# A decoder layer in a planned instruction order: rank-16 projection in two passes, attention weights on ScalarE's queue, and a revised planner

## Chip, core and metric

One Trainium2 chip, one of its NeuronCores. The metric is the device time of one execution in microseconds. The kernel before was run three times: 1096.41, 1093.22 and 1092.48 us, median 1093.22 us. The profiled execution is a separate one.

## What is computed

The input is `x` (8 sequences of 512 tokens, 256 features) and a context of the same shape. Each of three sublayers is followed by a residual sum and a layernorm, cut here to what matters:

```python
# 1: chunked linear attention, chunks of 32, with a gate
S = einsum(Qc, Kc) * decay_mask;  O = einsum(S, Vc)
x = layernorm(x + (sigmoid(x @ W_g.T) * O @ W_o.T + x))
# 2: cross attention, 16 heads of 64, 512 queries on 512 keys
a = softmax((x @ Wq + bq)(ctx @ Wk + bk).T / 8);  o = a @ (ctx @ Wv + bv)
x = layernorm(x + o @ Wo + bo)
# 3: feed-forward with ternary weights and a rank-16 side path
h = bitlinear(x, w_fc) + gate * (x @ v.T @ fast_b.T @ u.T)
x = layernorm(x + bitlinear(relu(h) ** 2, w_proj))
```

The rank-16 projection is `x @ v.T` (256 features to 16).

## The kernel before

**Precision.** Every float32 operand of a matmul is kept as two float16 tiles, a high part and the rest. A product is made in three passes, high by high, high by low and low by high (`PASSES`, line 35; `mm`, line 472). Making the two halves is the bulk of the work of the other engines: ScalarE (ACT) casts the high part and VectorE (DVE) subtracts it, with GpSimd (POOL) taking some of each.

**Units.** Cross attention is cut into 256 units: batch `b` (8), head pair `p` (8), query block `qt` (4 of 128 queries). `scores` (line 1025) makes one unit: six `s` matmuls of 512 columns in three concurrent pairs, a DVE instruction per head that adds the mask and finds the row's extreme (`s`, `nm`), and an ACT exponential per head (`e`). `split_pe` (line 1057) makes the two float16 halves of the 128x1024 probabilities: the high half on ACT, or on POOL where `HIGH` has a "p" for this `qt` (first string for batch 0, second for the others), and the low half on DVE (`ph`, both halves in one of three buffers). `split_p` (line 1045) sends `ph` through a transposing DMA on SyncE's (SP's) queue into `pT` (five buffers). `attend` (line 1067) comes `LAG` = 4 units later and multiplies `pT` by the values: 24 `av` matmuls of 64 columns. A `ph` buffer is free again when its transpose has landed.

**Work between the units.** Generators yield the other work piece by piece, and a budget per unit (`PULL`) says how much is taken: key, query and value projections for later head pairs (`pk`, `pq`, `pvv`), the first sublayer of the next batch (`gen_l0`, from line 772), the output projection and feed-forward of the batch before (`gen_wo`, line 883, `gen_ffn`, line 938). In batch 0 the last is replaced by the preparation of the feed-forward weights (`setup_wo`, `setup_ffn`). In the feed-forward, `ffn_z` (line 918) makes the rank-16 projection `pz`: six matmuls of 512 columns into 128 PSUM rows, of which `zst` is made; `ffn_h` (line 927) then adds `ust` by `zst` to each of eight hidden blocks. `vst` holds the 16 columns of `v.T` at columns 0, 32 and 64, a tile each for high and low.

**Before the first unit.** `load_w0`, `load_decay`, the inputs of batch 0 and `load_qkv` (line 560) are issued on SP's queue in that order. `wqs`, six tiles of 512 KB, are the cross attention's weights; `setup_qkv` splits each in a 256-column and a 768-column piece. `setup_decay` (line 535) builds the decay mask: `ld` on ACT and DVE, then eight powers `pw` on POOL, then four DVE instructions `mdec`. The first sublayer of batch 0 follows from `xh0`, the halves of the input (`xs`), and from `w0`.

**What sets the order.** All of it is recorded first. `schedule` (line 280) then plays the recorded operations through a model with a duration for each (`cost`, line 235), picks for each engine, at each moment, the ready operation with the lowest due time, and emits the program in that order. Due times are the unit's number plus an offset per kind of work (`LATE`). `REACH` says how far ahead in due time DVE may reach for an operation that does not wait for the SBUF port it shares with POOL. The order is fixed when the program runs: each engine takes its instructions one after the other, and an instruction that waits holds those behind it.

**Completion counters.** In the built program each DMA reports to one of eight completion counters, given out in turn, and a DMA that gets a counter again waits first for the DMA that had it before.

All instructions are emitted from one line (414 before), so a profile row is told by its tile names.

Of the kernel before, what the change touches and what calls it, by code (L numbers as in the profile page):

```python
# [15 lines left out]
ALU = mybir.AluOpType  # L16
# [9 lines left out]
PSC = 2.0 ** 15  # L26
LAG = 4
MARGIN = 0.0
REACH = 5.83
SPARE = 1  # L30
HIGH = ("aaaa", "paaa")
LATE = {"k": 0.0, "q": 0.0, "v": 0.0, "w": 0.0, "l": -0.81, "o": -0.22, "f": 0.0, "s": 0.0, "a": 1.41}
PULL = {"k": 4.02, "l": 2.62, "w": 3.0, "f": 4.71, "g": 6.03}

PASSES = ((0, 0), (0, 1), (1, 0))

# [90 lines left out]

class Op:
    __slots__ = ("engine", "method", "args", "kw", "prio", "seq", "preds", "succs", "wait", "occ", "lat", "half", "port",
                 "bufs", "start", "end", "free", "ready", "parts")  # L130


class Engine:
# [12 lines left out]
class Recorder:  # L146
# [34 lines left out]
    def add(self, engine, method, args, kw):  # L181
        ins, outs = [], []
        for n, x in enumerate(args):
            if isinstance(x, View):
                (outs if n == 0 or (method == "tensor_tensor_reduce" and n == 7) else ins).append(x)
        for k, x in kw.items():
            if isinstance(x, View):
                (outs if k == "accum_out" else ins).append(x)
        o = Op()
        o.engine, o.method, o.args, o.kw, o.prio = engine, method, args, kw, self.prio  # L190
        o.preds, o.succs, o.bufs, o.parts = {}, [], [], None
# [12 lines left out]
        return o  # L204
# [30 lines left out]
    def cost(self, o, ins, outs):  # L235

        n = max([int(np.prod(x.shape[1:])) for x in outs + ins] or [0]) if o.engine != "PE" else outs[0].idx.size
        psum = any(x.t.pool[:2] == "ps" for x in ins + outs)
        ones = sum(x.idx.size == 1 and x.t.free > 0 for x in ins)
        o.half, o.port = None, o.engine == "POOL"  # L240
        if o.engine == "PE":
            o.occ = n / 2400 + 0.0025
            o.lat = o.occ + 0.17
            if ins[0].p1 - ins[0].p0 == 64:
                o.half = ins[0].p0
        elif o.engine == "DVE":
            lat = 0.145 + n * 1.042e-3
            if o.method == "tensor_tensor_reduce":
                o.occ, o.lat = 0.615, 0.8
                return  # L250
            if not psum and o.method in ("tensor_copy", "tensor_scalar") and n >= 512:
                lat = 0.12 + n * 0.62e-3
            if psum and ones and o.method == "scalar_tensor_tensor":
                lat += 0.065
            if n <= 8:
                lat = 0.19 if o.method == "reciprocal" else 0.175 if o.method == "bn_aggr" else 0.145
            o.occ, o.lat = lat - 0.085, lat
            o.port = not psum and o.method in ("tensor_tensor", "scalar_tensor_tensor", "tensor_scalar", "tensor_copy")
        elif o.engine == "ACT":
            lat = 0.165 + n * 0.83e-3 + (0.0 if psum else 0.04) + 0.07 * ones  # L260
            o.occ, o.lat = (lat + 0.01, lat + 0.12) if "accum_out" in o.kw else (lat - 0.11, lat)
        elif o.engine == "POOL":
            if o.method == "tensor_tensor":
                lat = 0.3 + n * 1.67e-3 if n <= 512 else 0.2 + n * 1.9e-3
                if o.args[3] == ALU.pow:
                    lat = 0.42 + 0.16 * n
            else:
                lat = 0.13 + n * 0.9e-3 if n > 512 else 0.62 if n > 256 else 0.56 if n > 8 else 0.22 + n * 5e-3
            o.occ, o.lat = lat - 0.03, lat
        else:  # L270
            x = (outs or ins)[0]
            if o.method == "dma_start_transpose":
                blocks = n / 128
                o.occ, o.lat = 0.1 * blocks + 0.4, 0.115 * blocks + 0.55
            else:
                size = {F32: 4, F16: 2}.get(x.t.dt, 1)
                o.occ, o.lat = 0.6, n * size * x.shape[0] / 200e3


    def schedule(self):  # L280
# [18 lines left out]
        dma, halved = 0.0, False  # L299
        port = {"DVE": 0.0, "POOL": 0.0}  # L300
        times = [0.0]
        for o in ops:
# [14 lines left out]
        while done < len(ops):  # L317
# [10 lines left out]
            while again:  # L328
                again = False
                for e in engines:  # L330
# [35 lines left out]
                    if e == "PE":  # L366
# [1 line left out]
                        st = now + (0.095 if halved and not grouped else 0.0)  # L368
                        halved = grouped
                        o.free, o.end = st + o.occ, st + o.lat  # L370
                    elif e == "SP":
                        st = max(now, dma - 1.5)
                        dma = max(st, dma) + o.lat
                        o.free, o.end = st + o.occ, max(dma, now + o.lat) + 2.1
                    else:
                        st = now
                        if o.port:
# [58 lines left out]
def decoder_kernel(ctx: ExitStack, tc: tile.TileContext, ins: dict, out: bass.AP):  # L436
# [26 lines left out]
    tfc = cst.tile([128, 2, HID], F16, name="tfc")  # L463
    tpj = cst.tile([128, 8, D], F16, name="tpj")
    ust = cst.tile([128, HID], F16, name="ust")
    vst = cst.tile([128, 2, 2, 128], F16, name="vst")
    sfc4 = cst.tile([128, 8], F32, name="sfc4")
    s2b = cst.tile([128, D], F32, name="s2b")
    bob = cst.tile([128, D], F32, name="bob")
# [129 lines left out]
    def setup_ffn():  # L599
# [445 lines left out]
    def split_p(u, e):  # L1045
# [148 lines left out]
    for i, u in enumerate(units):  # L1194
        b, p, qt = u
        if qt == 0:
# [17 lines left out]
        at(i, 0)  # L1214
        step(u)
        at(i, LATE["a"])
        while len(pend) >= LAG:
# [101 lines left out]
```

## Time and profile before

| | profiled execution |
|---|---|
| own time | 1087.98 us |
| span, first to last instruction | 1086.2 us |
| TensorE (PE) busy | 1016.7 us, 94%, 11986 matmuls |
| DVE busy | 995.6 us, 92% |
| ACT busy | 896.4 us, 83% |
| POOL busy | 542.0 us, 50% |
| DMA | 185.81 MB, mean 171 GB/s |
| mean granted PE clock | 0.991 |

The profiled execution took 1.8 us more than its span and 5.2 us less than the median of the three timed runs. Busy shares are means over stages with different limits. A matmul row's mean duration includes its pipeline; how fast matmuls follow each other is seen in rows such as `pk x6`, six of 512 columns in 1.29 us of the chain.

Stages can be told along the matmul row by counting `s` matmuls, 192 to a batch. The first unit's scores start at 49.4 us, those of batch 1 at 173.3, batch 2 at 298.9, batch 3 at 422.8, batch 4 at 548.7, batch 5 at 671.9, batch 6 at 797.4 and batch 7 at 920.2; the last unit's at 1032.2 us, and the span ends at 1086.2.

### The profile page before, as it was taken

The page shows a single profiled execution, that of the slowest core. Times are in us where ns is not written, and L with a number is a line of the kernel's source. Part 1 is how long each engine was busy: PE and PEld are TensorE (multiplying, and loading weights), DVE is VectorE, ACT ScalarE, POOL GpSimd, SP SyncE. Part 2 cuts the span into 40 slices and gives each one's busy share as a digit, 9 for nine tenths or more (in the row PEclk, how much of TensorE's full clock was granted, in tenths as well). Part 3 has the DMA queues.
Part 4 walks back from the last instruction along what each step waited for, and adds up shares of the span by engine and source line. Part 5 has one row for each costly group of instructions (what it writes and reads, how often), then busy time and mean ns, then how long its engine had stood idle before and what let it go on. Part 6 is the DMA issues. An engine that isn't in the chain of part 4 may idle for free.

```text
span 1086.2 us, 30429 instructions
## 1 busy us (share of the span) xinstructions
PE 1016.7 (94%) x11986; PEld 641.1 (59%) x11986; DVE 995.6 (92%) x2105; ACT 896.4 (83%) x1871; POOL 542.0 (50%) x508
## 2 busy tenths in 40 slices
PE   6987879999999999999999999999999999999976
PEld 4544545666566666665666665665666666564654
DVE  6999899999899989999898989999898999996987
ACT  6788788789877998789987898879987899788854
POOL 3332261256842587335951588435962567443335
PEclk9999999999999999999999999999999999999998
DMA  7389999999999999999999999999999999998961
GB/s 258 112 141 174 168 202 183 166 175 167 184 171 184 171 188 168 193 161 174 190 179 185 169 182 181 200 161 173 181 178 183 176 177 177 182 159 155 166 105 39
DMA packets 651791, 185.81 MB, mean 171 GB/s; under 512 B 633728, under 2 KB 646528, under 8 KB 651648
## 3 DMA queue, kind: packets, MB, share of 16 engines
q1 hardware_dynamic: 651648, 183.87, 94.8%
q8 instruction: 93, 1.52, 0.6%
q14 instruction: 50, 0.41, 0.1%
HBM read 21.04 MB, written 4.19 MB: 23 GB/s over the span
## 4 chain that ended last, share of the span: by engine, by line
PE 39%; DMA 19%; ACT 16%; DVE 15%; issue 5%; POOL 5%; SPq 1%; ACTq 0%; POOLq 0%; DVEq 0%
DMA pT<-ph 12%; PE s L414 7%; PE av L414 6%; ACT e L414 6%; PE pwo L414 5%; DVE ph L414 4%; DVE s L414 4%; PE pvv L414 3%; ACT ph L414 3%; PE ph L414 3%; DMA x2T<-xsb 3%; PE pq L414 3%; ACT r L414 3%; PE pk L414 3%; DMA oT<-oh 2%
## 5 line engine op out<-in xcount | busy, mean ns | idle before, releaser
L414 ACT ACTIVATE e<-s,nm 128x512 f32<-128x512 f32 x512 | 353.4, 697 | 79.9 <-DVE nm L414 72.2
L414 DVE CUSTOM_DVE_ANT_0 s<-s,mb 128x512 f32<-128x512 f32 x512 | 343.3, 707 | 30.2 <-PE s L414 25.9
L414 DVE SCALAR_TENSOR_TENSOR ph<-e,ph 128x1024 f16<-128x1024 f32 x256 | 336.9, 1317 | 20.5 <-ACT ph L414 15.8
L414 PEld LDWEIGHTS <-pT 128*128 128x128 f16 x6144 | 213.7, 98 | 94.8 <-issue 36.3
L414 PE MATMUL av<-v,pT 128*128 128x64 f16 x6144 | 233.4, 194 | 18.7 <-DMA pT<-ph 17.7
L414 ACT ACTIVATE ph<-e 128x1024 f16<-128x1024 f32 x200 | 214.2, 1073 | 25.5 <-DMA pT<-ph 20.8
L414 PE MATMUL s<-W 64*128 64x512 f16 x1536 | 219.7, 380 | 7.0 <-ACT e L414 4.8
L414 POOL TENSOR_SCALAR ph<-e 128x1024 f16<-128x1024 f32 x56 | 66.8, 1192 | 198.5 <-ACT e L414 157.9
L414 POOL TENSOR_TENSOR oh<-of,oh 128x512 f16<-128x512 f32 x63 | 90.9, 1442 | 120.1 <-ACT oh L414 117.1
L414 PEld LDWEIGHTS <-wqkv 128*128 128x128 f16 x768 | 67.7, 98 | 91.7 <-issue 31.5
L414 ACT ACTIVATION_READ_ACCUMULATOR e<-s,nm 128x1 f32 x512 | 108.6, 212 | 0.0
L414 PEld LDWEIGHTS <-W 64*128 64x128 f16 x1536 | 58.2, 94 | 80.7 <-issue 41.5
L414 POOL TENSOR_TENSOR rh<-r,rh 128x512 f16<-128x512 f32 x56 | 71.3, 1278 | 68.8 <-ACT rh L414 62.0
L414 PE MATMUL pk<-ctxh,wqkv 128*128 128x512 f16 x384 | 97.9, 379 | 2.1 <-POOL ctxh L414 0.9
L414 PE MATMUL pq<-x1T,wqkv 128*128 128x512 f16 x384 | 96.3, 383 | 3.7 <-ACT e L414 1.8
L414 PE MATMUL pvv<-wqkv,ctxh 128*128 128x256 f16 x768 | 96.1, 273 | 1.2 <-ACT e L414 1.2
L414 PE MATMUL pwo<-wo,oT 128*128 128x256 f16 x672 | 87.6, 273 | 3.4 <-DMA oT<-oh 3.4
L414 PEld LDWEIGHTS <-ctxh 128*128 128x128 f16 x768 | 70.8, 98 | 30.2 <-issue 17.6
L414 PEld LDWEIGHTS <-oT 128*128 128x128 f16 x768 | 70.7, 98 | 19.1 <-DMA oT<-oh 5.8
L414 DVE DVE_READ_ACCUMULATOR2_ANT nm<- 128x1 f32 x512 | 72.1, 141 | 0.0
L414 PE MATMUL ph<-x2T,tfc 128*128 128x512 f16 (+1 forms) x288 | 70.5, 361 | 0.1
L414 PE MATMUL py<-tpj,rh 128*128 128x256 f16 x448 | 60.6, 273 | 0.1
(186 smaller groups left out, 1501.3 us busy)
## 6 DMA issues: line engine op xcount, KB each, us to landing
row<-in_x SPq DMA_DIRECT2D x8, 512.0 KB, 5.4
pT<-ph SPq DMA_TRANSPOSE x255, 4.8
xs<-in_xT SPq DMA_DIRECT2D x7, 512.0 KB, 4.8
ctxs<-in_ctxT SPq DMA_DIRECT2D x7, 512.0 KB, 4.8
out_dram<-row SPq DMA_DIRECT2D x7, 512.0 KB, 3.4
wqs<-in_wqkv SPq DMA_DIRECT2D x6, 512.0 KB, 7.0
wos<-in_wo SPq DMA_DIRECT2D x4, 256.0 KB, 3.3
fcs<-in_w_fc SPq DMA_DIRECT2D x2, 512.0 KB, 4.2
```

The lines of the kernel that those rows point to most:

```text
L414: getattr(real[x.engine], x.method)(*[r(a) for a in x.args], **{k: r(a) for k, a in x.kw.items()})
```

## The change

1. `ffn_z`: `vst` becomes one tile with the high part of `v.T` at columns 0, 32 and 64 and the low part at 96. Each 128-column weight tile meets the high and the low half of the input once: four matmuls in place of six. `fbs`, from which `ust` is made, is copied to rows 96 too, so that the fourth group of 16 rows is summed in the same `ust` by `zst` matmul.
2. `load_qkv`: the six `wqs` transfers are issued by ACT's queue in place of SP's.
3. `HIGH` for batch 0: "papa" in place of "aaaa": the high half of `ph` is made on POOL for two of four query blocks.
4. The planner: new durations for DMAs and for one POOL operation, a limit of eight transfers in flight per queue, and new values of `REACH`, `LATE` and `PULL`. The transposes of `ph` get a due time of their own (`d`). Several new offsets are zero.

```diff
-REACH = 5.83
+REACH = 8.03
-HIGH = ("aaaa", "paaa")
-LATE = {"k": 0.0, "q": 0.0, "v": 0.0, "w": 0.0, "l": -0.81, "o": -0.22, "f": 0.0, "s": 0.0, "a": 1.41}
-PULL = {"k": 4.02, "l": 2.62, "w": 3.0, "f": 4.71, "g": 6.03}
+HIGH = ("papa", "paaa")
+LATE = {"k": 0.0, "q": 0.0, "v": 0.0, "w": 0.0, "l": -0.41, "o": -0.91, "f": 0.31, "s": 0.0, "a": 1.41, "t": 0.0, "x": 0.0, "e": 0.0, "c": 0.0, "d": -1.17}
+PULL = {"k": 4.02, "l": 2.62, "w": 3.05, "f": 4.71, "g": 6.26}
...
+        o.dma = o.method[:3] == "dma"
+        if o.dma:
+            x = (outs or ins)[0]
+            if o.method == "dma_start_transpose":
+                blocks = n / 128
+                o.occ, o.lat = 0.1 * blocks + 0.4, 0.115 * blocks + 0.55
+            else:
+                size = {F32: 4, F16: 2}.get(x.t.dt, 1)
+                o.occ, o.lat = 0.45, n * size * x.shape[0] / 300e3 + (1.2 if size == 1 else 0.1)
...
-                lat = ... 0.62 if n > 256 else ...
+                lat = ... 0.92 if n == 256 and o.kw == {} and o.method == "tensor_scalar" and o.args[-1] == ALU.is_lt else 0.62 if n > 256 else ...
...
-                o.occ, o.lat = 0.6, n * size * x.shape[0] / 200e3
...
-                    elif e == "SP":
-                        st = max(now, dma - 1.5)
+                    elif o.dma:
+                        st = max(now, landed[e][-8])
+                        if o.method == "dma_start_transpose":
+                            st = max(st, dma - 1.5)
                         dma = max(st, dma) + o.lat
-                        o.free, o.end = st + o.occ, max(dma, now + o.lat) + 2.1
+                        o.free, o.end = st + o.occ, max(dma, st + o.lat) + 2.2
+                        landed[e].append(o.end)
...
-    vst = cst.tile([128, 2, 2, 128], F16, name="vst")
+    vst = cst.tile([128, 2, 128], F16, name="vst")
...
-            nc.sync.dma_start(st, ins["wqkv"][i, c * 128:(c + 1) * 128])
+            nc.scalar.dma_start(st, ins["wqkv"][i, c * 128:(c + 1) * 128])
...
-        split(vst[:, :, 0, 0:RANK], vst[:, :, 1, 0:RANK], sv, WS)
+        split(vst[:, :, 0:RANK], vst[:, :, 96:96 + RANK], sv, WS)
         for g in (32, 64):
-            nc.vector.tensor_copy(vst[:, :, :, g:g + RANK], vst[:, :, :, 0:RANK])
+            nc.vector.tensor_copy(vst[:, :, g:g + RANK], vst[:, :, 0:RANK])
...
-        for g in (32, 64):
+        for g in (32, 64, 96):
             nc.vector.tensor_copy(fbs[:, :, g:g + RANK], fbs[:, :, 0:RANK])
...
-        mm(ps, lambda k, a: vst[:, k, a, :], lambda k, c: x2T[b][:, c, k, ts], 2)
+        for k in range(2):
+            for c in range(2):
+                nc.tensor.matmul(ps, vst[:, k, :], x2T[b][:, c, k, ts], start=(k == 0 and c == 0), stop=(k == 1 and c == 1))
...
+            nc.prio += LATE["d"]
             nc.sync.dma_start_transpose(t.rearrange("p a h k n -> p (a h k) n"), ph.rearrange("p a h n -> p (a h n)"))
+            nc.prio -= LATE["d"]
```

More of the change, by code (lines that the diff above doesn't have):

```diff
@@ L129 @@
     __slots__ = ("engine", "method", "args", "kw", "prio", "seq", "preds", "succs", "wait", "occ", "lat", "half", "port",
-                 "bufs", "start", "end", "free", "ready", "parts")
+                 "dma", "bufs", "start", "end", "free", "ready", "parts")
 class Engine:
@@ L190, in add @@
         o.engine, o.method, o.args, o.kw, o.prio = engine, method, args, kw, self.prio
+        if engine in ("DVE", "ACT") and method[:3] != "dma" and self.prio >= 0:
+            src = ins[0].t if ins else None
+            if method == "tensor_tensor_reduce":
+                o.prio += LATE["t"]
+            elif method == "activation" and args[2] == AF.Exp:
+                o.prio += LATE["x"]
+            elif src is not None and src.pool[:2] == "ps":
+                o.prio += LATE["e"]
         o.preds, o.succs, o.bufs, o.parts = {}, [], [], None
@@ L240, in cost @@
         o.half, o.port = None, o.engine == "POOL"
-        if o.engine == "PE":
+        o.dma = o.method[:3] == "dma"
[7 more added lines that the diff above has]
+                o.occ, o.lat = 0.45, n * size * x.shape[0] / 300e3 + (1.2 if size == 1 else 0.1)
+        elif o.engine == "PE":
             o.occ = n / 2400 + 0.0025
@@ L267, in cost @@
             else:
-                lat = 0.13 + n * 0.9e-3 if n > 512 else 0.62 if n > 256 else 0.56 if n > 8 else 0.22 + n * 5e-3
+                lat = 0.13 + n * 0.9e-3 if n > 512 else 0.92 if n == 256 and o.kw == {} and o.method == "tensor_scalar" and o.args[-1] == ALU.is_lt else 0.62 if n > 256 else 0.56 if n > 8 else 0.22 + n * 5e-3
             o.occ, o.lat = lat - 0.03, lat
[L270 to L276, printed above, removed]
-                o.occ, o.lat = 0.6, n * size * x.shape[0] / 200e3
     def schedule(self):
@@ L298, in schedule @@
         future = {e: [] for e in engines}
-        dma, halved = 0.0, False
+        dma, halved, landed = 0.0, False, {"SP": [0.0] * 8, "ACT": [0.0] * 8}
         port = {"DVE": 0.0, "POOL": 0.0}
@@ L1214, in decoder_kernel @@
         at(i, 0)
+        nc.prio = i + LATE["c"]
         step(u)
```

## Prediction

> **What bounds the kernel now.** I read the page's busy line and chain first, then the busy time of each engine by batch, the chain inside two batches, the waits of batch 0, and the timeline of the first 51 us.
>
> ```profile
> PE 1016.7 (94%) x11986; PEld 641.1 (59%) x11986; DVE 995.6 (92%) x2105; ACT 896.4 (83%) x1871; POOL 542.0 (50%) x508
> PE 39%; DMA 19%; ACT 16%; DVE 15%; issue 5%; POOL 5%; SPq 1%; ACTq 0%; POOLq 0%; DVEq 0%
> ```
>
> No engine has slack to speak of except POOL, and the chain is shared by four. So a microsecond saved on one engine is worth less than a microsecond.
>
> ```profile
> 0.00:49.40 49.40, 38.63 (x271) 24.16 (x273) 38.84 (x82) 32.29 (x63) 17.36 (x25) 1.00 0.62 204
> 49.40:173.30 123.90, 101.14 (x1182) 57.99 (x1182) 114.53 (x255) 101.74 (x219) 42.26 (x41) 0.97 0.97 166
> 298.90:422.80 123.90, 123.09 (x1481) 78.13 (x1478) 117.19 (x244) 106.29 (x223) 70.46 (x63) 1.00 1.04 178
> ```
>
> The columns are length, then busy time of PE, PEld, DVE, ACT and POOL, granted clock, DMA share and rate. Batch 2 is PE's: busy 123.1 of 123.9. Batch 0 is as long though PE is idle for 22.8 us in it; there DVE is nearest to full (114.5). The next lines show why, first the chain in batch 2, then in batch 0, then two waits of batch 0.
>
> ```profile
> 337.01 0.76 PE s L414 x6
> 337.76 1.40 PE pq L414 x6
> 339.16 1.29 PE pg L414 x6
> ```
> ```profile
> 56.73 6.37 DMA pT<-ph
> 63.18 1.06 ACT ph L414
> 70.92 6.25 DMA pT<-ph
> 77.25 1.06 ACT ph L414
> ```
> ```profile
> ACT ph L414 <- DMA pT<-ph: 7.2, 8, 1.5
> DVE ph L414 <- ACT ph L414: 3.4, 5, 1.1
> ```
>
> In batch 2 matmul follows matmul. In batch 0 a transpose of 6.4 us ends and an ACT cast starts: the cast needs one of three `ph` buffers, and ACT, waiting for it, holds its later exponentials. Last, the start:
>
> ```profile
> 0.72 1.28 ACT L414 ACT_TABLE_LOAD   x1 [0.72 <-PEq L1312]
> 5.20 0.20 ACT L414 ACTIVATE ld<-ld 128x1 f32<-128x1 f32 x1 [3.20 <-DMA ld<-in_log_decay]
> 5.77 8.73 POOL L414 TENSOR_TENSOR pw<-ld,dif 128x4 f32<-128x4 f32 x8 [4.95 <-DMA dif<-in_diffmask]
> 10.32 4.08 SPq L414 DMA_DIRECT2D wqs<-in_wqkv  x6
> 14.53 0.77 DVE L414 SCALAR_TENSOR_TENSOR mdec<-pw,dif 32x32 f32<-32x32 f32 x4 [1.96 <-POOL pw L414]
> 50.91 0.70 DVE L414 CUSTOM_DVE_ANT_0 s<-s,mb 128x512 f32<-128x512 f32 x1
> ```
>
> DVE waits 1.96 us for the decay powers and then works nearly without a stop to the first unit's scores at 50.91.
>
> **Two passes for three.** Fourteen matmuls of 512 columns go (two in each of seven batches) and four of 256. In the chain `pg x6` takes 1.29 us, so 0.215 each; half for 256. 14 x 0.215 + 4 x 0.108 = 3.4 us of PE. It counts in full where PE is the chain and not where DVE is: between 3.4 and nothing. Batches 1 to 6, where `pz` runs, are PE's by the table, so I take 2.6, three quarters. The extra copy of `fbs` is one DVE instruction of about 0.1 us, the smaller `vst` copies save less; nothing. If the cover of DVE work that stays (117.2 of 123.9 in batch 2) is the tighter bound, the term is zero.
>
> **The weights on ACT's queue.** Each issue costs about 0.5 us of an engine's queue (three `w0s` in 1.46 us of SP's timeline), so six leave SP and come to ACT, which has nothing to do before 5.20. The splits of `wqs`, between 18.85 and 43 us before, come first in ACT's new order, and the six pieces they feed on DVE go into DVE's idle time at the start: 10.6 us of idle in 49.4. That is the promise. Against it stands what is queued behind. In the changed order ACT issues the six first, then loads its table, then casts `wqs`, then `wqkh`, and only after five such casts `ld`. The built program gives its eight completion counters out over both queues, so ACT's sixth issue waits until the third `wqs` has landed, its fourth until `wqk` has, and SP's second `xs` until the first `wqs` has.
>
> When does the third `wqs` land? The first 20 us moved 293 GB/s at a DMA share of 0.86, so about 341 when full. `wqk`, 256 KB, took 3.1 us from issue to landing (the page's DMA list), of which 0.8 is its bytes: 2.3 fixed. Three `wqs` are 1.57 MB; with what SP issued beside them (two `wqk`, one `xs`) 2.36 MB. So it lands at 0.72 + 2.3 + 4.6 = 7.6 if ACT's transfers go first, 9.9 if all share. Another issue (0.5) and the table load (1.28) put ACT's first cast at 9.4 to 11.7, where `ld` was done at 5.20. From there DVE has 4.5 us of lower halves ahead of `ld` (five pieces of `wqs` and two of `wqkh` at their rows' durations) with 0.4 to start; then POOL's powers take 8.73, and `mdec` can start 13.7 after the first cast: 23.1 to 25.4. From `mdec` to the first unit's scores DVE has 67 instructions, 28.8 us at the rows' durations; before, the 70 there were 33.1 us of work in 36.4 us of time, so 3.3 were lost. I allow 2.7: 31.5. First scores at 54.6 to 56.9, against 50.91. In exchange 0.8 us of DVE work (`bob`, `fbs`) is done that came later before. The term is +2.9 to +5.2; I take +4. If the counters hold nothing and ACT starts at 5.2, the same sum gives 18.9 + 31.5 - 0.8 = 49.6: -1.3, the other end.
>
> Here a rule of the Trainium skill speaks against the edit. The rows just used say that the transfers of the start are limited by bytes: 5.9 MB in the first 20 us. "DMA: Bandwidth & Descriptors", section "Issuing engines are not separate DMA queues", says that DMAs run on the same 16 engines whoever starts them, and that issuing from several saves only the issue time. By the rule the landing would be the later of my two, the term +5.2 and the sum -0.7. The trace of before cannot show how two queues share, since only SP's was used.
>
> **POOL's casts in batch 0.** Sixteen high halves leave ACT (32.56 us for 31 casts in batch 0, so 1.05 each: 16.8 us of its 101.7) and come to POOL at 1.19 each (the `ph` row of POOL, 66.8 us for 56): 19.1 on 42.3, of 123.9, so POOL has room. ACT does not bound batch 0; DVE does, with 9.4 us idle. What ACT gains is that a cast waiting for a buffer waits on POOL, where nothing urgent is behind: half of 7.2 us of ACT's waits, and with them part of DVE's 3.4 for ACT. I take -3. The best is all of DVE's idle, -9.4. The worst: the cast is 0.14 us longer, 16 times 2.2, and DVE's `ph`, 37.25 us for 31 in batch 0 and 42.31 for 33 in batch 2, where POOL is busier, is stretched by 0.08 in 32 units, 2.6: +4.8.
>
> **Durations and dates.** In a middle batch the new order differs in 18 of DVE's 243 instructions, 9 of ACT's 158, 2 of POOL's 63 and 1 of SP's 47; the PE work between a unit's scores and its `av` is 17.3 us on average in both. So nothing structural moves. What such swaps do is bounded by what the kernel shows without any: batches 2 to 6, in one and the same order, took 122.8 to 125.9. I take 0, and 3.5 either way over the seven. In the tail (54.0 us) four short matmuls go and a few casts swap: -0.3. In the transposes' due time `d` I see no separate term: SP's order differs in one place of a batch.
>
> **Sum.** +4 - 2.6 - 3 + 0 - 0.3 = -1.9. Span 1086.2 to 1084.3, own time of the profiled execution 1087.98 to 1086.1, and of the median, which is 5.2 above that own time, 1093.2 to 1091.3.
>
> **Rivals.** (1) *Batch 0 gives up all its slack.* If the ring of three buffers with ACT in it is what keeps DVE at 114.5 of 123.9, taking ACT out of half the casts frees all 9.4 instead of 3: -8.3, 1084.9. For it: the transposes fill the chain of batch 0. Against: transposes still take 6.4 us and there are still three buffers.
> (2) *POOL holds DVE.* Both share a port to SBUF in the planner's model, and the timeline has a DVE `ph` of 1.93 us at 610.87 where 1.22 is usual. If each of 16 new POOL casts cost 0.71 on DVE, batch 0 would lose 11.4 instead of gaining 3: +12.5, 1105.7. It decides from the first cast on, since the other terms leave +1.1; at half the casts the time is 1100.0. Against it: nine `ph` of DVE that overlapped a POOL cast of `ph` alone took 1.21 to 1.22.
> (3) *The start is not held.* Term -1.3 in place of +4: -7.2, 1086.0. Against: the waits stand in the program.
> That the edit does not do what it says can be left out: the new program has 18 matmuls fewer, 16 more casts on POOL and six DMAs on ACT.
>
> **How the numbers follow.** 0.5% of 1093.2 is 5.5 us, about what a measurement here can tell from no change. The forecast, within that, with all terms between their bounds: 0.52. Faster by more: rival 1 at 0.16, rival 3 at 0.08, and a lucky sum of swaps (2.6 becomes 3.4, swaps -3.5: -6.2) 0.06, together 0.30. Slower by more: rival 2 at 0.08, and the start at its upper end with the cast's worst (+5.2 + 4.8 - 2.9 = +7.1) at 0.10, together 0.18. The forecast's own range is 1087.8 to 1098.7. The range for 8 in 10 reaches down to 1083, a little past rival 1, and up to 1100, the last sum.
>
> **What would show it.** Right: ACT's first cast near 9 to 12 us instead of 5.2, the first `s` of DVE near 55, `pw` ending near 23; batch 0 shorter by some 3 us with less ACT waiting for `pT`; two matmuls fewer in a middle batch and its length shorter by 0.4. Wrong: `ld` on ACT before 8 us, DVE's `ph` in batch 0 above 1.3 us on average, or middle batches that change by more than 1 us each.

## The result, and the profile after

The changed kernel took 1096.66 us (median of 20 runs, 1092.5 to 1103.22), the kernel before 1091.77 beside it on the same chip (20 runs, 1088.3 to 1096.7). The ratio is 1.0048, with an interval of 1.0031 to 1.0065: slower by half a per cent, where 1.9 us of gain had been forecast. The profiled execution took 1093.21 us, its span is 1091.4 us and its granted clock 0.991, as before.

The page of the changed kernel, busy time of each engine and the chain by engine:

```profile
PE 1011.3 (93%) x11968; PEld 642.1 (59%) x11968; DVE 989.5 (91%) x2106; ACT 881.7 (81%) x1855; POOL 558.3 (51%) x524
PE 39%; DVE 22%; DMA 17%; ACT 10%; issue 7%; POOL 4%; SPq 1%; DVEq 0%; ACTq 0%; POOLq 0%
```

PE, DVE and ACT all work less than before, by 5.4, 6.1 and 14.7 us, and the span is 5.2 us longer. The work went down; the waiting went up. (The 5.2 us are one trace against one: a second trace of the kernel before, in the table below, also has a span of 1091.4. That the change is slower rests on the 20 runs of each.) The next lines are the windows of the start, batch 0 and batch 2 of the changed kernel (columns as in the prediction):

```profile
0.00:59.30 59.30, 39.93 (x286) 26.01 (x287) 41.57 (x88) 32.79 (x63) 20.53 (x29) 1.00 0.52 170
59.30:179.10 119.80, 98.46 (x1155) 57.38 (x1155) 115.64 (x250) 88.17 (x205) 60.14 (x53) 0.97 0.98 175
303.00:427.50 124.50, 122.51 (x1477) 77.72 (x1476) 115.53 (x244) 106.74 (x223) 71.03 (x63) 1.00 1.02 180
```

The first unit starts 9.9 us later than before (59.3 against 49.4), batch 0 is 4.1 us shorter, and batch 2 is 0.6 longer although it has two matmuls fewer (single batches of the two traces of the kernel before differ by as much). The timeline of the start shows why the first is so late:

```profile
0.72 10.14 ACTq L426 DMA_DIRECT2D wqs<-in_wqkv  x6
10.88 1.28 ACT L426 ACT_TABLE_LOAD   x1 [10.88 <-DMA dif<-in_diffmask]
12.18 1.15 ACT L426 ACTIVATE wqkv<-wqs 128x256 f16<-128x256 f32 x2
15.62 0.19 ACT L426 ACTIVATE ld<-ld 128x1 f32<-128x1 f32 x1
17.21 9.61 POOL L426 TENSOR_TENSOR pw<-ld,dif 128x4 f32<-128x4 f32 x8 [16.39 <-DVE ld L426]
26.84 2.42 DVE L426 SCALAR_TENSOR_TENSOR mdec<-pw,dif 32x32 f32<-32x32 f32 x4 [1.27 <-POOL pw L426]
60.36 0.69 DVE L426 CUSTOM_DVE_ANT_0 s<-s,mb 128x512 f32<-128x512 f32 x1
```

ACT issues six transfers from 0.72 to 10.86 us and can do nothing else meanwhile. `ld`, done at 5.2 before, is done at 15.6, and everything after it follows.

Lengths in us, told along the matmul row as in the section on the profile before, for the executions that the text uses ("rest" runs from the last unit's scores to the end of the span):

| kernel | start | batch 0 | batch 1 | 2 to 6 | batch 7 | rest | span |
|---|---|---|---|---|---|---|---|
| before | 49.4 | 123.9 | 125.6 | 621.3 | 112.0 | 54.0 | 1086.2 |
| before, second trace | 50.1 | 123.7 | 125.8 | 624.2 | 113.7 | 53.9 | 1091.4 |
| after | 59.3 | 119.8 | 123.9 | 625.4 | 110.1 | 52.9 | 1091.4 |
| e5_papa | 50.4 | 125.7 | 123.2 | 615.4 | 113.1 | 53.0 | 1080.8 |
| e16_ph_moved_32_bytes | 49.4 | 123.4 | 126.1 | 617.6 | 112.9 | 53.2 | 1082.6 |
| h1_before_512 | 50.0 | 118.8 | 119.8 | 611.7 | 110.5 | 52.9 | 1063.7 |
| h5_two_pass_512 | 49.4 | 119.7 | 119.5 | 611.3 | 108.5 | 55.9 | 1064.3 |
| h4_two_pass_new_plan_512 | 47.6 | 124.4 | 120.5 | 615.9 | 106.6 | 53.4 | 1068.4 |
| h3_new_plan_papa_sp_512 | 46.6 | 123.7 | 120.9 | 613.9 | 106.7 | 53.7 | 1065.5 |
| h2_after_512 | 59.4 | 116.9 | 121.4 | 617.3 | 106.7 | 54.3 | 1076.0 |
| h6_papa_512 | 49.6 | 123.7 | 120.0 | 612.9 | 108.7 | 53.1 | 1068.0 |

### The profile page after: what moved, and what is told of

Read it like the earlier page. It is cut to its first block, busy times and chain, and to the rows that moved or that the text cites. A ratio compares the mean times of both kernels' runs of the same rounds, so it can differ in the third digit from the quotient of the medians.

```text
span 1091.4 us, 30392 instructions
## 1 busy us (share of the span) xinstructions
PE 1011.3 (93%) x11968; PEld 642.1 (59%) x11968; DVE 989.5 (91%) x2106; ACT 881.7 (81%) x1855; POOL 558.3 (51%) x524
## 4 chain that ended last, share of the span: by engine, by line
PE 39%; DVE 22%; DMA 17%; ACT 10%; issue 7%; POOL 4%; SPq 1%; DVEq 0%; ACTq 0%; POOLq 0%
DMA pT<-ph 7%; PE s L426 7%; DVE s L426 7%; DVE ph L426 6%; PE av L426 6%; PE pwo L426 5%; PE ph L426 4%; PE pk L426 3%; ACT e L426 3%; DMA oT<-oh 3%; PE pq L426 3%; DMA x2T<-xsb 3%; PE pvv L426 3%; ACT ph L426 2%; DVE W L426 2%
## 5 line engine op out<-in xcount | busy, mean ns | idle before, releaser
L426 DVE SCALAR_TENSOR_TENSOR ph<-e,ph 128x1024 f16<-128x1024 f32 x256 | 328.4, 1284 | 14.4 <-ACT ph L426 10.7
L426 PEld LDWEIGHTS <-pT 128*128 128x128 f16 x6144 | 216.8, 98 | 89.0 <-issue 38.7
L426 PE MATMUL av<-v,pT 128*128 128x64 f16 x6144 | 237.3, 193 | 16.2 <-DMA pT<-ph 15.1
L426 POOL TENSOR_SCALAR ph<-e 128x1024 f16<-128x1024 f32 x72 | 86.3, 1198 | 295.8 <-ACT e L426 212.6
L426 ACT ACTIVATE ph<-e 128x1024 f16<-128x1024 f32 x184 | 197.1, 1071 | 24.4 <-issue 11.8
L426 PEld LDWEIGHTS <-W 64*128 64x128 f16 x1536 | 58.1, 94 | 79.6 <-issue 39.0
L426 ACT CAST oh<-of 128x512 f16<-128x512 f32 x63 | 39.8, 632 | 30.5 <-POOL ph L426 14.7
```

The lines of the kernel that those rows point to most:

```text
L426: getattr(real[x.engine], x.method)(*[r(a) for a in x.args], **{k: r(a) for k, a in x.kw.items()})
```

## The experiments

Every ratio below is against the kernel before, run beside it on the same chip; its median was 1089.4 to 1091.8 us in the six sets of runs.

### One part at a time

**e1_sp_queue**, the changed kernel with the weights back on SP's queue.

```diff
-            nc.scalar.dma_start(st, ins["wqkv"][i, c * 128:(c + 1) * 128])
+            nc.sync.dma_start(st, ins["wqkv"][i, c * 128:(c + 1) * 128])
```

> The changed kernel with the six weight transfers back on SP's queue; the planner then makes its own start and batch 0, batches 2 to 7 keep the changed order. Theory A (the transfers on ACT's queue made the start long): first scores at 49 to 52 us instead of 59.3, the rest as in the changed kernel, so 8 to 10 us less than it and 3 to 5 us less than before (ratio to before 0.995 to 0.998). Rival B (the start is long because the new planner puts the weight splits early, whoever issues the transfers): first scores at 56 to 60, ratio to before 1.002 to 1.005. Rival C (a late start is made up again later, and the loss is in the middle batches): first scores early, but the time within 2 us of the changed kernel.

Measured: 1.0008 (0.9992 to 1.0023), first unit at 47.2 us. The start comes back 12 us, and 4.4 us of time come back with it. But the rest of the change, which was forecast to gain 5.9 us, gains nothing: the start is earlier than theory A had it, and the time lies between A and C.

**e2_three_on_act**, three of the six weights on ACT's queue, three on SP's.

```diff
-            nc.scalar.dma_start(st, ...)
+            (nc.scalar if (i, c) in ((1, 0), (1, 1), (0, 0)) else nc.sync).dma_start(st, ...)
```

> The changed kernel with the first three weight transfers on ACT's queue and the other three on SP's; three issues need no completion counter that is in use, so ACT goes on at once, while the bytes and nearly the same cast order stay. Theory A1 (ACT is held at its issues by completion counters): ACT's first cast at 5 to 7 us instead of 12.2, first scores at 51 to 55 instead of 59.3, 4 to 8 us less than the changed kernel. Rival A2 (the bytes of the weights and their place in ACT's order hold the first sublayer): first cast early, but first scores at 57 to 60 and the time within 2 us of the changed kernel.

Measured: 0.9993 (0.9973 to 1.0014), first unit at 51.3 us, 0.0055 below the changed kernel: theory A1. ACT's three issues end at 2.11 us where the six ended at 10.86, and its first cast starts at 4.64 instead of 12.18.

**e4_two_pass**, the kernel before with two passes only (the edits of `vst`, `fbs` and `ffn_z` from the change).

> The kernel before with the projection in two passes alone; the order is otherwise the same but for single instructions. By the prediction's term: 2.6 us less than before (ratio 0.9976), middle batches 0.4 shorter each. Rival (DVE is the tighter bound in the middle): 0 to 1 us less. Rival (the whole PE saving counts, and more through the latency of the projection): 3.4 to 5 us less.

Measured: 1.0042 (1.0025 to 1.006). Less work on PE and a slower kernel: none of the three expectations.

**e5_papa**, the kernel before with one string changed.

```diff
-HIGH = ("aaaa", "paaa")
+HIGH = ("papa", "paaa")
```

> The kernel before with half of batch 0's high halves on POOL alone; only batch 0 is planned anew. By the prediction's term: batch 0 at 121 us instead of 123.9 and 3 us less in all (ratio 0.997). Rival (POOL's casts hold DVE): DVE's ph in batch 0 above 1.5 us on average and 3 to 11 us more. Rival (the 4 us that batch 0 lost in the changed kernel came from the planner's new durations, or from work done in its longer start, not from POOL): batch 0 within 1 us of 123.9 and the time within 1.5 us of before.

Measured: 0.9953 (0.9934 to 0.9973). Faster, by more than the 0.997 of the forecast, and not where it was forecast: batch 0, the only one whose casts the edit moves, is 1.8 us longer in the trace, and batches 2 to 6, whose instructions stand in the same order as before, are 5.9 us shorter together.

**c0_same_kernel**, the kernel before against itself.

> The kernel before, unchanged, measured as if it were another kernel. It leaves nothing out. Theory A (a trace repeats): ratio 0.9985 to 1.0015, each of batches 2 to 6 within 0.4 us of its length in the first trace (123.9, 125.9, 123.2, 125.5, 122.8), and the same casts of ph on DVE take 1.9 us or more again, among them the one 33.9 us into batch 3. Rival B (the waits between DVE and POOL are dealt anew in each execution): the ratio is the same, but single batches move by 1 us or more and the long casts are others; then no batch length of a single trace may be read closer than that.

Measured: 0.9994 (0.9977 to 1.0012). Rival B as far as single batches go: the second trace moves them by up to 1.1 us (batches 2 to 6: 124.1, 126.9, 123.8, 125.7, 123.7), so the middle of `e4_two_pass` (626.3 us) is not told apart from it; the 5.9 us of `e5_papa` is beyond it on both traces.

**e9_two_pass_old_order**, two passes with every engine's order kept.

```diff
+                    if x in self.drop:
+                        continue
...
+                o = nc.tensor.matmul(ps, vst[:, k, a, :], x2T[b][:, c, k, ts], start=(n == 0), stop=(n == 4))
+                if a:
+                    nc.drop.add(o)
```

> The kernel before with the rank-16 projection in two passes, but every engine's order kept exactly as before (the planner is shown three passes, and the third pass's matmuls are dropped when the program is written out). Against e4_two_pass, which cost 1.0042, only the 1 to 11 swapped DVE instructions of a batch are undone. Theory A (the swaps cost it): 0.9965 to 0.999, middle batches 0.4 us shorter each. Rival B (not the swaps but when DVE and POOL meet at SBUF; a shift of some tenths of a us deals it anew): anything between 0.995 and 1.005, and DVE's time above its usual durations in batches 1 to 6 changes by about as many us as the batches do (21.7 us before, 26.8 in e4_two_pass). Rival C (the two passes themselves are dearer, in the copy of zst or the projection behind it): 1.003 to 1.005, with the lost time ahead of zst or ph.

Measured: 1.0027 (1.0008 to 1.0045), with the end of the trace 4 us longer (58.1). Theory A is out, and B holds as far as the time goes: swapped instructions explain at most a part of `e4_two_pass`.

**e7_old_start_no_papa**, the changed kernel with "aaaa" in batch 0 and the weights on SP's queue.

> The changed kernel with the weights back on SP's queue and the casts of batch 0 back on ACT: two passes and the new durations and dates are left of the change. Theory A (the parts add up, as measured so far: papa 0.9953 alone): e1_sp_queue's 1.0008 with papa taken out, 1.0055, and then the new plan is worth 1.0055 against two passes alone at 1.0042: nothing or a little worse. Rival B (papa gains only where the old plan left DVE and POOL in each other's way): 0.999 to 1.002. Rival C (the new plan gains 2 us or more by itself): below 1.002 with batches 2 to 6 shorter than in e4_two_pass by over 0.4 us each.

Measured: 1.0131 (1.0101 to 1.0162), the slowest of all, and outside every expectation. Putting papa into it (which gives `e1_sp_queue`) gains 1.2%, where papa in the old plan gained 0.5%. Parts that do not add up say that something else changes with them. The next section finds 0.6% of it; another 0.6% of the step from `e7_old_start_no_papa` to `e1_sp_queue` stays unexplained.

**e10_papa_three_act**, papa and three weights on ACT's queue in the kernel before.

> The kernel before with the papa casts of batch 0 and three of the six first weights through ACT's queue, three passes and the old durations (the planner is told that ACT may issue DMAs). Theory A (the parts add up: papa 0.9953, three on ACT 0.9985 against six on SP): 0.994, 1083.5. Rival B (what the start gains or loses is made up in batch 0, and the moment of arrival in batches 1 to 6 decides): 0.993 to 1.000 with no relation to the first scores' time. First scores at 49 to 53 us in both.

Measured: 0.9993 (0.9975 to 1.0011). They do not add up here either; of the two theories only B's wide range holds it.

### What changed with them: the place of `ph`

In the built programs of `before` and `e5_papa` nearly all places of buffers start at the same byte of a partition (93 of 96). Papa makes the third `ph` buffer's first writer come one step earlier, so it lies below a 32-byte buffer instead of above it: at 209408, a multiple of 512, in place of 209440. All three `ph` buffers of `before`, `e4_two_pass`, `e7_old_start_no_papa` and `e9_two_pass_old_order` lie 32 bytes off a multiple of 64; in `after`, `e1_sp_queue`, `e2_three_on_act`, `e5_papa` and `e10_papa_three_act` one of the three is on a multiple of 512. Three experiments move buffers and leave every instruction in its order.

**e16_ph_moved_32_bytes** and **e13_papa_ph_at_old_place**: the third `ph` is placed before its small neighbour in the first, after it in the second.

```diff
+        if key == "nm_2" and key not in self.seen and "ph_2" not in self.seen:
+            self.seen.add("ph_2")
+            self.pools[pool].tile([128, 2, 2, T], F16, tag="ph_2", name="early", bufs=1)
```

> The kernel before with one change of place and none of order: the third ph buffer lies 32 bytes lower (byte 209408 of a partition, a multiple of 64, in place of 209440), and a buffer of 32 bytes that lay below it lies above it. This is the one difference in place that papa made by the way in e5_papa, where transposes from that buffer took 3.3 us and from the other two 3.9 to 4.1, and where 7,487 packets of 256 bytes took 40 to 43 ns in place of 11,588. Theory A (where ph lies sets what its transposes cost): 0.9955, as e5_papa, with about 7,500 such packets and 3.3 us for a third of the transposes. Rival B (papa gained because POOL casts in ACT's place): 0.998 to 1.002 here.

> e5_papa (the kernel before with papa in batch 0) in exactly its order, but the third ph buffer put back at the place it had in the kernel before, 32 bytes higher. Theory A (the place made the gain): 0.998 to 1.002, about 11,500 packets of 40 to 43 ns. Rival B (POOL's casts made it): 0.9953 as in e5_papa. A mixture of both would show in this run and e16_ph_moved_32_bytes sharing the 0.0047.

Measured: 0.9942 (0.992 to 0.9964) and 1.0027 (1.0006 to 1.0048). Thirty-two bytes make all of what papa seemed to gain; papa itself loses a little (its interval just clears 1).

**e12_all_on_64_bytes** and **e14_after_on_64_bytes**: padding so that each buffer starts at a multiple of 64.

```diff
+            if self.at[pool] % 64:
+                self.pools[pool].tile([128, 8], F32, name=f"pad_{key}")
```

> The kernel before in exactly its order, every buffer in SBUF starting at a multiple of 64 bytes (padding of 32 bytes where needed; nothing else). Before, all three ph, all five pT, all eight oT and 7 W, row, xs buffers start 32 bytes off. Theory A: three thirds of what one buffer of ph brings, 14 us, 0.987, with service of a transpose near 3.3 us for all; if destinations and loads matter too, more. If DVE or PE takes over as the bound, half of it, 0.993. Rival B (place plays no part): 0.998 to 1.002.

> The changed kernel in exactly its order, every buffer in SBUF starting at a multiple of 64 bytes. It has one of three ph buffers there already (byte 208896). Theory A: two thirds of 14 us less than the changed kernel's 1.0048, so 0.996, and 0.009 slower than e12_all_on_64_bytes, which would be what the change costs when places are the same. If DVE or PE takes over, 1.000. Rival B: 1.003 to 1.006.

Measured: 0.9809 (0.9782 to 0.9836) and 0.9938 (0.9917 to 0.9959). The first is below what three `ph` buffers would bring, so other places count too. Both times are below what theory A gave. The two kernels now stand 1.3% apart.

**h1_before_512**: small buffers first, then padding, then all others, each on a multiple of 512.

```diff
+        for pool, n in at.items():
+            if n % 512:
+                self.pools[pool].tile([128, (512 - n % 512) // 4], F32, name=f"pad_{pool}")
```

> The kernel before in exactly its order, every buffer of 512 bytes or more starting at a multiple of 512 bytes (small ones placed together first, then padding). In e12_all_on_64_bytes two ph buffers lay on 512 bytes and their transposes took 4.5 us from issue to landing, the third on 128 and took 4.9. Theory A (it takes 512): about 4.5 for all three and 0.978 to 0.980. Rival B (64 is enough, the third is slow for another reason): 0.980 to 0.982, third buffer again near 4.9.

Measured: 0.9777 (0.9759 to 0.9796), 1065.46 us. It beats both kernels, with the order of the one before. Its five runs lie between 1065.25 and 1066.64 us, where the kernel before varied by 4.8 to 8.5 us in each set of 9 to 32 runs. (Not every kernel below is as steady: their four or five runs vary by 0.9 to 5.2 us.) The lists of DMAs of `before`, `e16_ph_moved_32_bytes` and `h1_before_512` follow in this order: packets, MB and share of the DMA engines' time, then the transposes with their median from issue to landing in us.

```profile
q1 hardware_dynamic: 651648, 183.87, 94.8%
pT<-ph SPq DMA_TRANSPOSE x255, 4.8
```
```profile
q1 hardware_dynamic: 651648, 183.87, 92.4%
pT<-ph SPq DMA_TRANSPOSE x255, 4.6
```
```profile
q1 hardware_dynamic: 651648, 183.87, 86.1%
pT<-ph SPq DMA_TRANSPOSE x255, 4.0
```

Packets and bytes are the same to the last one; the time that they take is not. Counted in the traces' packet records, 22,566 of 619,520 packets of 256 bytes took 40 to 43 ns before, 16,700 with one `ph` moved, 260 on 512; the usual packet takes 18. (These packets are the plainest sign, and about a third of the time saved.) By buffer, mean from issue to landing in batches 2 to 6 (53 or 54 transposes each): before 5.03, 5.11 and 5.10 us; in `e16_ph_moved_32_bytes` 5.04, 5.14 and, for the moved one, 4.53; in `e12_all_on_64_bytes` 4.53 and 4.49 for the two on 512 and 4.89 for the third, which is on 128; in `e14_after_on_64_bytes` 4.53, 4.47, and 4.93 for the one on 64; in `h1_before_512` 4.45, 4.41 and 4.26. Theory A held: a multiple of 64 or 128 is not enough. Where the transposes write seems to matter little: all `pT` buffers lay 32 bytes off in `e16_ph_moved_32_bytes` and on 512 in `e12_all_on_64_bytes`, and a `ph` on 512 gave 4.5 us in both.

The Trainium skill has a rule for this, "DMA: Bandwidth & Descriptors", section "How a descriptor splits into AXI transactions": a transaction has to start at a multiple of 256 bytes, and a piece that starts elsewhere begins with one from the boundary below it. By that rule a 256-byte piece 32 bytes off takes two transactions in place of one. The runs agree in direction (5.0 to 5.1 us off, 4.3 to 4.5 on); no run here had a `ph` buffer on a multiple of 256 that was not one of 512.

### The parts again, at equal places

With all large buffers on 512, the change was put together step by step: `h1_before_512`, two passes (`h5_two_pass_512`), the new durations and dates (`h4_two_pass_new_plan_512`), papa (`h3_new_plan_papa_sp_512`), the weights on ACT's queue (`h2_after_512`). The edits are those above.

> e9_two_pass_old_order (two passes, every engine's order as before) on the same 512-byte places. Theory A (two passes save what PE saves once transposes are no longer in the way): 0.002 to 0.003 below h1_before_512. Rival B (they cost, as in e9_two_pass_old_order): 0.001 to 0.004 above it, with the tail 2 to 4 us longer. Rival C: within 0.001 of it, since DVE and the transposes set the end.

Measured: 0.9789 (0.9768 to 0.9809), 1066.39 us, 0.0012 above `h1_before_512`, and their intervals overlap. It lies just past C and at the lower end of B, whose longer end it shows; A is out.

> e7_old_start_no_papa (two passes, new durations and dates; weights on SP's queue, casts of batch 0 on ACT) on the same 512-byte places. Theory A (the new order of instructions itself costs, as e7_old_start_no_papa against e4_two_pass: 1.0131 against 1.0042): 0.006 to 0.010 above h5_two_pass_512. Rival B (that cost came from where its buffers lay, not from the order): within 0.002 of h5_two_pass_512.

Measured: 0.9826 (0.9807 to 0.9845), 1071.36 us, 0.0037 above `h5_two_pass_512`. Between A and B: the order itself costs some two fifths of what `e7_old_start_no_papa` showed over `e4_two_pass` (0.0089).

> The changed kernel in exactly its order on the same 512-byte places. Theory A (places hid part of the change's cost): 0.011 to 0.015 above h1_before_512, as e14_after_on_64_bytes stood 0.0129 above e12_all_on_64_bytes; so 0.989 to 0.994. Rival B (at equal places the change costs what it seemed to, 0.0048): 0.982 to 0.985. First scores near 60 us as in the changed kernel.

Measured: 0.9892 (0.9873 to 0.9912), 1077.87 us, 0.0115 above `h1_before_512`. Theory A.

> e1_sp_queue (the changed kernel with its first weights back on SP's queue) on the 512-byte places. It stands between h4_two_pass_new_plan_512 (0.9826, 1071.36: without papa) and h2_after_512 (0.9892, 1077.87: with ACT's queue), which lie 6.5 us apart. Theory A (the start costs it, since first scores come 12 us later and batch 0 gives half back): 0.983 to 0.985, so papa 0 to 2 and the start 4 to 6. Rival B (papa costs it, DVE held by POOL in batch 0): 0.987 to 0.989, batch 0 over 3 us longer than in h4_two_pass_new_plan_512.

Measured: 0.9829 (0.9804 to 0.9853), 1071.69 us: papa 0.0003, the weights' queue 0.0063. Theory A, with the start a little past it. (Its profiled execution, 1067.36, was the lowest of its four; the table's row is that one.)

> e5_papa (the kernel before with papa in batch 0 only) on the 512-byte places, against h1_before_512 (0.9777, 1065.46). Theory A (papa by itself costs 1 to 4 us, as e13_papa_ph_at_old_place, 1.0027, against the kernel before): 0.979 to 0.981, batch 0 longer and DVE's casts of ph in batch 0 above 1.3 us on average. Rival B (papa gains 2 us or more once its place is not in question): below 0.976.

Measured: 0.9817 (0.9799 to 0.9835), 1069.76 us, 0.0040 above `h1_before_512`. Theory A, a little past its end.

## Why the prediction was wrong, point by point

A difference of two ratios here is good to about 0.003, or 3 us (each interval is 0.002 either way). So only the weights' queue, the place of `ph`, the order and papa in the old plan stand clear of zero, the last two just so. The parts were put together in one sequence only; in another they may come out otherwise. With ratios turned into us by 1091.8:

| term | forecast, us | measured, us | from |
|---|---|---|---|
| weights on ACT's queue | +4 (-1.3 to +5.2) | +6.9 | h2 - h3 |
| two passes | -2.6 (-3.4 to 0) | +1.3 | h5 - h1 |
| papa | -3 (-9.4 to +4.8) | +0.3 in the new plan, +4.4 in the old | h3 - h4, h6 - h1 |
| durations and dates | 0 (-3.5 to +3.5) | +4.0 | h4 - h5 |
| end of the span | -0.3 | not measured by itself | in the rows above |
| place of the third `ph` | not seen | -6.3 | e16 |
| sum | -1.9 | +6.2 | measured directly +5.2 |

**The term that was not there.** No step asked where buffers lie. The change moves one `ph` from 32 bytes off to a multiple of 512, which by itself is worth 6.3 us, and so hides more than half of what the change costs: 12.5 us (0.0115) at equal places, 5.2 as built. The row that would have raised the question was on the page: the transposes' 4.8 us, and a DMA share of 0.97 and 1.04 in the two batches that the prediction showed, and it used neither.

**Two passes: the step that failed is "Batches 1 to 6 ... are PE's by the table".** The busy column was taken for the bound. Here are batch 4 of `h1_before_512` and batches 3 and 4 of `h5_two_pass_512`:

```profile
533.80:656.30 122.50, 122.35 (x1484) 78.03 (x1482) 115.89 (x244) 106.64 (x223) 72.48 (x63) 1.00 0.96 182
```
```profile
411.00:533.50 122.50, 122.19 (x1482) 77.94 (x1480) 115.88 (x244) 106.65 (x223) 72.45 (x63) 1.00 0.91 183
533.50:655.90 122.40, 122.18 (x1478) 77.77 (x1476) 115.79 (x244) 106.53 (x223) 72.46 (x63) 1.00 0.97 182
```

Two matmuls are gone, 0.43 us of issue, and the batch keeps its length to 0.1 us; over batches 2 to 6 it is 611.7 against 611.3. PE is still shown busy for all but 0.2 us, but a matmul row's duration includes its pipeline and so reaches over short waits. Read by the starts of the matmuls in the traces, PE does stand still: the steps that are over 0.1 us longer than usual for their kind add up to 4.0 us of excess in batch 4 of `h1_before_512` and 4.2 in that of `h5_two_pass_512`. The bound of zero, named for the case that other work sets the end, was the value. What sets 122.4 instead was not settled: every engine repeats the same pattern, DVE with 116 us. What the two traces show beside it sits at the end: batch 7 is 2.0 us shorter and the rest 3.0 longer, where PE's clock is at half for longer (17.1 us after the last unit's scores, against 11.8). The windows of 12 us that lie 24 us after the last unit's scores, of `h1_before_512` and `h5_two_pass_512` (the third number from the right is the clock):

```profile
1034.80:1046.80 12.00, 12.00 (x103) 10.21 (x102) 8.49 (x21) 6.29 (x18) 7.84 (x11) 0.92 0.13 46
```
```profile
1032.40:1044.40 12.00, 11.62 (x83) 9.20 (x84) 7.88 (x20) 6.18 (x17) 5.63 (x9) 0.73 0.13 46
```

That the clock falls there is seen in all traces. How long it stays down does not go with the two passes alone: 15.5 to 20.6 us in the three kernels with two passes and the old plan against 12.0 before, but 16.2 in `e13_papa_ph_at_old_place` with three passes, and 10.6 and 11.4 in `h3_new_plan_papa_sp_512` and `h4_two_pass_new_plan_512` with two. What sets it is open.

**The weights on ACT's queue: ACT was held at its issues as forecast, but the wait that ended last was another, and three sizes were off.** The forecast put the first cast at 9.4 to 11.7, `mdec` at 23.1 to 25.4, and first scores at 54.6 to 56.9; they came at 12.18, 26.84 and 60.36. The step that failed is "ACT's sixth issue waits until the third `wqs` has landed". That one landed at 8.44, inside the forecast's 7.6 to 9.9, and would have put the first cast at 10.2. But ACT's fifth issue took over the counter of `dif`, a 32 KB transfer on SP's queue which the forecast did not look at, and could not start before `dif` landed at 10.01 us (the row of ACT's table load above names it as what ended the idle time). The rows of `dif` in the two DMA lists, before and after (the last number is us from issue to landing):

```profile
dif<-in_diffmask SPq DMA_DIRECT2D x1, 32.0 KB, 3.4
```
```profile
dif<-in_diffmask SPq DMA_DIRECT2D x1, 32.0 KB, 7.8
```

From the first cast to `mdec` it took 14.7 us instead of 13.7 (the eight powers took 9.61 us, not 8.73), and from there 33.5 instead of 31.5 (`mdec` alone 2.42 instead of 0.77, while POOL's casts and subtractions of the input ran beside it). So the start is 12.8 us longer than with SP's queue (59.4 against 46.6 at equal places), where the forecast had 4 to 6 over the kernel before. The credit was too small as well: 0.8 us was counted for work done early, while DVE did 41.6 us of work before the first scores where it did 37.9, and batch 0 gave back 6.8 us (123.7 to 116.9). The Trainium skill's rule cited in the prediction, from "DMA: Bandwidth & Descriptors", section "Issuing engines are not separate DMA queues", spoke for the later landing. The trace has the two queues sharing, as the rule says: in the median, `wqs` took 5.8 us from issue to landing instead of 7.0, but SP's `wqk` beside them 6.0 instead of 3.1; the third `wqs` landed between the forecast's two times.

**Papa: right about the wait, wrong about what it is worth.** The step that failed is that shorter waits of ACT shorten batch 0 by 3 us. ACT's waits for a `ph` buffer did fall, from 7.2 us to 1.9 in batch 0:

```profile
ACT ph L426 <- DMA pT<-ph: 1.9, 3, 1.3
```

Aligned buffers take most of them away without papa (2.5 us in `h1_before_512`). And POOL, now busier, holds DVE: rival 2, at a third of its price. The groups of DVE's low halves in batch 0, of `h1_before_512` and of `h6_papa_512` (mean ns before the second bar):

```profile
L443 DVE SCALAR_TENSOR_TENSOR ph<-e,ph 128x1024 f16<-128x1024 f32 x31 | 38.0, 1233 | 0.9 <-ACT ph L443 0.6
```
```profile
L443 DVE SCALAR_TENSOR_TENSOR ph<-e,ph 128x1024 f16<-128x1024 f32 x30 | 40.0, 1340 | 0.2 <-ACT ph L443 0.2
```

Thirty times 0.107 is 3.2 us of batch 0's 4.9. The casts of `ph` themselves hardly do it: of these 30, one starts while such a cast runs, with 0.13 us of it left, and is not longer. Six start while a POOL instruction with two inputs runs, and together they are 3.5 us longer than usual; in `h1_before_512` it is three and 0.1 us. The casts push those instructions to other moments. In the timeline of `h6_papa_512` one starts 0.02 us ahead of a `ph`:

```profile
125.92 1.16 POOL L443 TENSOR_TENSOR oh<-of,oh 128x512 f16<-128x512 f32 x1 [1.26 <-ACT oh L443]
125.94 2.22 DVE L443 SCALAR_TENSOR_TENSOR ph<-e,ph 128x1024 f16<-128x1024 f32 x1
```

DVE takes 2.22 us where it takes 1.22: it waits until POOL is all but done. A cast that runs first does the same, as in the timeline of the changed kernel, where 0.52 us of one are left:

```profile
1011.52 1.05 POOL L426 TENSOR_SCALAR ph<-e 128x1024 f16<-128x1024 f32 x1
1012.05 1.59 DVE L426 SCALAR_TENSOR_TENSOR ph<-e,ph 128x1024 f16<-128x1024 f32 x1 [2.60 <-ACT ph L426]
```

So the forecast's evidence against rival 2, nine casts on POOL that cost DVE nothing, did not bear on it: in all nine DVE had started first. In the new plan, with its own order, papa neither gains nor costs anything that can be measured. The mark set in the prediction (above 1.3 us means rival 2) was not reached in the changed kernel, whose mean in batch 0 is 1.273, and it was reached in the old plan.

**Durations and dates: the step that failed is the bound of 3.5 us.** Plus or minus 3.5 us came from how much batches of one order differ. That is the noise of an order, not a bound on what another order costs. Counting swapped instructions said "nothing structural"; at equal places the new order costs 4.0 us (5.0 between the medians of the two sets of runs), at the old places more (1.0131 against 1.0027 and 1.0042 for two passes without the new durations and dates: 10 to 11 us). Batch 3 of `h4_two_pass_new_plan_512`, against 122.50 above:

```profile
415.10:540.30 125.20, 122.73 (x1477) 77.90 (x1476) 115.45 (x244) 107.03 (x223) 70.16 (x63) 1.00 0.93 178
```

Batches 3 and 5 are 2.8 and 1.8 us longer, batches 2, 4 and 6 within 0.4, and batch 0 by 4.7; the start, batch 7 and the end give 1.8, 1.9 and 2.5 back. Which of the swaps does it is open.

**The numbers.** The forecast's sign was wrong; range and result were not far apart: 1.0048 of 1093.2 is 1098.5, inside 1083 to 1100. But no case that it named is what happened: the start, the two passes and the new order all came out at or past the slow end of their bounds (by less than a difference here is good to), papa gained nothing, and only the unseen -6.3 brought the time that near. That the range holds it is luck.

## What to carry to other kernels

Before costing an edit, look at where the buffers of frequent DMAs lie, and look again in the edited program: an edit that allocates one small buffer earlier or later can move large ones off or onto a boundary, and here one such move was worth 6.3 us, about as much as the largest part of the change. Put such buffers on multiples of 512 first, and measure edits after that. A busy share near 100% does not make an engine the bound: take a known piece of its work away and see whether the stage gets shorter.

## What the runs showed of the hardware that was not expected

- A transposing DMA's source 32 bytes off a multiple of 64 takes 5.0 to 5.1 us from issue to landing here, on a multiple of 64 or 128 alone 4.9, on 512 4.3 to 4.5; the whole kernel is 2.2% faster with all large buffers on 512, with the same instructions in the same order.
- An engine that issues DMAs is held by them: six transfers took 10.14 us of ACT's time at the start, three of them 1.39, where SP's queue had taken 4.08 for the same six later on. The difference is waiting for completion counters, the last of them for a transfer of 32 KB on the other queue.
- A POOL instruction that starts ahead of a two-input one on DVE can make it wait nearly to its end: a `ph` on DVE took 2.22 us instead of 1.22 behind one with two inputs, and 1.59 behind a cast with 0.52 us left.
- Two traces of one kernel differ by up to 1.1 us in a batch of 125; on aligned buffers, batches 2, 4 and 5 came out at 122.4 or 122.5 us in both `h1_before_512` and `h5_two_pass_512`.
